# Moving the stores of an inverse transform from GpSimd's queue to SyncE's

## The chip, the cores and the metric

The kernel runs on one core of a Trainium2 chip. The metric is the device time of one execution in microseconds, and the time given is the median of several executions. Profiles are of one execution each. In their rows PE is TensorE's matmul, PEld its weight load, DVE is VectorE, ACT is ScalarE, POOL is GpSimd and SP is SyncE; SP does no arithmetic and serves to issue transfers.

## The reference

The input x has 16 samples of 16 channels of 256 x 256 float32. Four layers follow each other, and each adds a convolution of the normalised input to the input (normalised: by group of two channels, over a sample).

```python
x = x + _L0_conv_ref(_gn(x), L0_conv_weight)      # 3x3, circular
x = x + _L1_conv_ref(_gn(x), L1_conv_filter_w)    # 5 taps on a diagonal
x = x + _L2_conv_ref(_gn(x), ty, tx, pole1, pole2, residue)
x = x + _L3_conv_ref(_gn(x), w_int8, scale, bias) # 3x3 on quantised input
```

Layer 2 is the one that matters here. It takes a 2-D Fourier transform of its input, mixes the channels at every frequency, transforms back, and adds a second term that is made of exponentials of learned poles over the two axes:

```python
alpha = jnp.fft.fft2(x, axes=(-2, -1))
output_residue1 = jnp.einsum('biox,oxik->bkox', alpha, S)
x1 = jnp.fft.ifft2(output_residue1, s=(Ny, Nx), axes=(-2, -1)).real
F = jnp.einsum('kbpq,bipz->kbiqz', output_residue2, E1)
x2 = jnp.einsum('kbiqz,biqx->kizx', F, E2).real
return x1 + x2 / Nx / Ny
```

Layer 3 quantises its normalised input by the largest absolute value of the whole tensor, so that nothing of it can start before all of layer 2's result is known.

## The kernel before

The program runs in stages, and each keeps its result in DRAM for the next: layers 0 and 1 (result `x2d`), the forward transform, the mixing of channels (result `mixd`), the inverse transform (result `x3d`, which is the sum of `x2d` and layer 2), and layer 3 (result `out`). The change is in the inverse transform.

That stage has 128 iterations. The outer loop runs over pairs of channels (`k` = 0, 2, ... 14), the inner one over the 16 samples `b`; one iteration makes one sample's two output channels, 128 partitions of 4 rows of 256. Numbered through, iteration n is `k` = 2 (n // 16), `b` = n % 16. The steps of an iteration are:

- `ot` (L1111): the mixed frequencies of eight samples, loaded at every eighth iteration by 16 transfers of 256 KB on SP's queue; two buffers.
- `xt` (L1118): the part of `x2d` to which the result is added, one transfer of 512 KB on SP's queue; four buffers.
- `along_y` (L1066): 64 small matmuls on PE into `ps_z` (three PSUM buffers), copied by ACT to `zt` (L1069).
- `ps_f` (L1123): one matmul with the exponentials, copied by ACT to `fs` (L1125).
- `along_x`, which PE does one iteration late, for the sample before: 32 matmuls into `ps_o` (L1078, L1079; three PSUM buffers), copied by ACT to `rq` (L1080; three buffers). From there POOL makes `w` (two operations) and half of `o`, DVE the other half (all of these are recorded at line L190, that of a helper). DVE then adds `o` into `xt` and keeps the largest value (`mx`, L1090), and takes statistics (`bn_stats` at L1094, `bn_aggr` at L1095) and the smallest value (`mn`, L1096).
- the store: POOL issues the transfer of `xt` to `x3d` (L1097), 512 KB.

The call `exponentials(k + 2)` stands in the program at `b` = 4 of each round of 16. It gives ACT, DVE and POOL (`dex`, `du`, `da`, `exp` in the rows) a few operations each, in the course of a round.

Only PE's order is written out by hand (`manual_schedule`). The order on the other engines and on SP's queue is made by a scheduler at build time, from the program's order and its own estimates. At run time every engine and every queue goes through its instructions in order: one that waits holds up all behind it. On SP that means loads of `ot` and of `xt` in one sequence. A load of `xt` can be issued when the store of four iterations before has landed, for it takes over that buffer.

After the last iteration the scales of layer 3 are made from the statistics (from L1138), and layer 3 loads `x3d` with SP (L1234) and stores `out` with POOL (L1270).

Of the kernel before, what the change touches and what calls it, by code (L numbers as in the profile page):

```python
# [57 lines left out]
P = 128  # L58
# [106 lines left out]
def layers(ctx, tc, x, w0, w1, w3, sw, bias, ty, tx, p1a, p1b, p1c, p2a, p2b, p2c, resa, resb,  # L165
           const, rows, out):
    nc = tc.nc
# [8 lines left out]
    x3d = [x3p[b // 2][b % 2] for b in range(B)]  # L176
# [12 lines left out]
    def tt(eng, o, a, b, op):  # L189
        eng.tensor_tensor(o, a, b, op)  # L190

    V, Q = nc.vector, nc.gpsimd
# [20 lines left out]
    def strip_weights(pool, src, taps, dtype, name, parts):  # L213


        raw = pool.tile([P, taps, C], F32, tag=f"{name}r", name=f"{name}r")
        nc.sync.dma_start(raw, src)
        n = sum(c for _, _, c, _ in parts)
        w = pool.tile([P, n, C * S], dtype, tag=name, name=name)
        for to, frm, count, m in parts:  # L220
            for i in range(count):
                tt(Q, w[:, to + i, :].rearrange("p (o s) -> p o s", s=S), bc(raw[:, frm + i, :], 2, S),
                   bc(strip[:, m, :], 1, C), MUL)
        return w
# [454 lines left out]
    with ExitStack() as es:  # L679
# [17 lines left out]
        with ExitStack() as tmp:  # L697
# [3 lines left out]
            for m, (t, pole) in enumerate(((ty, p1b), (tx, p2b))):  # L701
                rs = over_step(tp, t, f"b{m}")
                w = tp.tile([P, 2], F32, tag=f"wn{m}", name=f"wn{m}")
                V.tensor_scalar(w, nat, rs, TWO_PI, MUL, MUL)
                pr, pi, h = (tp.tile([P, C * KP], F32, tag=k, name=f"{k}{m}") for k in ("pr", "pi", "h"))
# [295 lines left out]
    with ExitStack() as es:  # L1001
# [28 lines left out]
        def exponentials(k):  # L1030


            made, turns = [], []
            for m in range(2):
                ex, u = (ap_.tile([P, 2, N], F32, tag=f"{n}{m}", name=f"{n}{m}") for n in ("dex", "du"))
                pr, pi = poles_[m]
                for d in range(2):
                    nc.scalar.activation(ex[:, d], times[m], AF.Exp, scale=pr[:, k + d : k + d + 1])
                    nc.scalar.activation(u[:, d], times[m], AF.Identity, bias=quarter, scale=pi[:, k + d : k + d + 1])
                turns.append((ex, u))  # L1040
            for m, (ex, u) in enumerate(turns):

                a = ap_.tile([P, 2, N], F32, tag=f"da{m}", name=f"da{m}")
                V.tensor_scalar(a, u, ROUND, ROUND, ADD, SUB)
                tt(Q, u, u, a, SUB)
                nc.scalar.activation(a, u, AF.Sin, scale=BELOW_TWO_PI)
                if m:
                    V.scalar_tensor_tensor(ex, ex, sign, a, MUL, MUL)
                else:
                    tt(V, ex, ex, a, MUL)  # L1050
                e = ep.tile([P, 2, 2, P], F32, tag=f"exp{m}", name=f"exp{m}")
                for s_, op_ in enumerate((ADD, SUB)):
                    tt(V, e[:, :, s_, :], ex[:, :, 0:P], ex[:, :, P:N], op_)
                made.append(e)
            return made
# [4 lines left out]
        def along_y(b, d, ot):  # L1060

            ps = ps_z.tile([P, 2, 2, P], F32, tag="ps_z", name="ps_z")
            for a, c in cells:
                for t in range(4):
                    r, half = t // 2, t % 2
                    nc.tensor.matmul(ps[32 * t : 32 * t + 32, a, c, :], lhsT=ot[:, a, d, 2 * c + half, r, b % BD],  # L1066
                                     rhs=inv[:, a, r], start=True, stop=True)
            zt = tp.tile([P, 2, 2, P], F32, tag="zt", name="zt")
            nc.scalar.copy(zt, ps)  # L1069
            return zt  # L1070

        def along_x(b, k, zts, fs, ey, xt):

            rq = rp.tile([P, 2, 2, 2 * P], F32, tag="rq", name="rq")
            for d in range(2):
                ps = ps_o.tile([P, 2, 2, P], F32, tag="ps_o", name="ps_o")
                for a, c in cells:
                    nc.tensor.matmul(ps[:, a, c, :], lhsT=zts[d][:, a, c, :], rhs=last[:, c, :], start=True, stop=False)  # L1078
                    nc.tensor.matmul(ps[:, a, c, :], lhsT=fs[:, d, a, :], rhs=ey[:, d, c, :], start=False, stop=True)  # L1079
                nc.scalar.copy(rq[:, d], ps.rearrange("p a c x -> p a (c x)"))  # L1080
            w = zp.tile([P, 2, 2, 2 * P], F32, tag="w", name="w")
            for h, op_ in enumerate((ADD, SUB)):
                tt(Q, w[:, :, h], rq[:, :, 0], rq[:, :, 1], op_)
            o = zp.tile([P, 2, 2, 2, P], F32, tag="o", name="o")
            parts_ = w.rearrange("p d h (c x) -> p (d h) c x", c=2)
            for h, (eng, op_) in enumerate(((V, ADD), (Q, SUB))):
                tt(eng, o[:, :, :, h, :].rearrange("p d h x -> p (d h) x"), parts_[:, :, 0], parts_[:, :, 1], op_)
            at = b * (C // 2) + k // 2
            flat = xt.rearrange("p d h w -> p (d h w)")
            V.tensor_tensor_reduce(flat, flat, o.rearrange("p d h c x -> p (d h c x)"), 1.0, -3.0e38, ADD, ALU.max,  # L1090
                                   mx3[:, at : at + 1])
            st = small.tile([P, 2, 6], F32, tag="st3", name="st3")
            for d in range(2):
                V.bn_stats(st[:, d], xt[:, d].rearrange("p h w -> p (h w)"))  # L1094
            V.bn_aggr(mv3[:, at, :], st.rearrange("p d s -> p (d s)"))  # L1095
            V.tensor_reduce(mn3[:, at : at + 1], flat, AX.X, ALU.min)  # L1096
            Q.dma_start(x3d[b][k : k + 2].rearrange("c (h p) w -> p c h w", p=P), xt)  # L1097

        with tc.manual_schedule(engines={mybir.EngineType.PE}):
            before = None  # L1100
            exps = exponentials(0)
            for k in range(0, C, 2):
                for b in range(B):
                    if b % BD == 0:

                        ot = op.tile([P, 2, 2, 4, 2, BD, 32], F32, tag="ot", name="ot")
                        for a in range(2):
                            for d in range(2):
                                for r in range(2):
                                    for u in range(2):  # L1110
                                        nc.sync.dma_start(  # L1111
                                            ot[64 * u : 64 * u + 64, a, d, :, r].rearrange("p t b g -> p t (b g)"),
                                            mixd[64 * a : 64 * a + 64, :, k + d, (r + u) % 2, u, b : b + BD]
                                            .rearrange("q t b g -> q t (b g)"))
                    if b == 4:
                        coming = exponentials(k + 2) if k + 2 < C else None
                    xt = xp.tile([P, 2, 2, N], F32, tag="xt3", name="xt3")
                    nc.sync.dma_start(xt, x2d[b][k : k + 2].rearrange("c (h p) w -> p c h w", p=P))  # L1118
                    zts = [along_y(b, d, ot) for d in range(2)]

                    fs = fp.tile([P, 2, 2, P], F32, tag="fs", name="fs")
                    ps = ps_f.tile([P, 512], F32, tag="ps_f", name="ps_f")
                    nc.tensor.matmul(ps, lhsT=gall[:, b, :], start=True, stop=True,  # L1123
                                     rhs=exps[0].rearrange("p k a y -> p (k a y)"))
                    nc.scalar.copy(fs.rearrange("p k a y -> p (k a y)"), ps)  # L1125
                    if before:
                        along_x(*before)
                    before = (b, k, zts, fs, exps[1], xt)
                    if k == C // 2 and b == 0:
                        wt = strip_weights(last_, w3, 9, BF16, "wt3", [(0, 0, 9, 0), (9, 0, 3, 1), (12, 6, 3, 2)])  # L1130
                exps = coming
            along_x(*before)


        tp = es.enter_context(tc.tile_pool(name="d_s", bufs=1))
# [248 lines left out]
```

## Time and profile before

| what | us |
|---|---|
| runs: median (lowest, highest) | 4475.6 (4469.8, 4476.33) |
| profiled execution, its own time | 4466.67 |
| its span in the profile | 4464.9 |
| first start of the store at L1097 | 3154.8 |
| last start of the store at L1097 | 4053.1 |
| busy in the whole span: PE | 3986.4 |
| busy in the whole span: DVE | 3051.8 |
| busy in the whole span: ACT | 2752.2 |
| busy in the whole span: POOL | 2208.0 |

The median of the runs and the profiled execution are of different executions of the same program; what is worked out from the profile is to be set against the profile's own time. A share of busy time over the whole span is a mean over five stages with different limits, and what is read for one stage has to be taken from a window on that stage. Times within the profile count from the start of the span. "x3d<-xt" in a row means that the instruction writes `x3d` and reads `xt`.

### The profile page before, as it was taken

How to read it: one execution, taken by the hardware profiler on the slowest of the kernel's cores; microseconds unless marked ns; L12 is line 12 of the kernel's file. 1: busy time of each engine (PE TensorE's matmuls, PEld its weight loads, DVE VectorE, ACT ScalarE, POOL GpSimd, SP SyncE). 2: the span in 40 equal slices, each digit the busy share in tenths (PEclk: the TensorE clock that was granted, in tenths of full speed). 3: DMA queues.
4: the chain of work that ended last, by engine and by line, in shares of the span. 5: the costliest groups of instructions: out<-in, count | busy, mean ns of one | idle time of the engine just before them, and what ended most of it. 6: DMA issues, size and time to landing. Idle time of an engine off the chain costs nothing. (4 is left out here: it accounts for less than half of the span.)

```text
span 4464.9 us, 122570 instructions
## 1 busy us (share of the span) xinstructions
PE 3986.4 (89%) x50800; PEld 3069.6 (69%) x50800; DVE 3051.8 (68%) x5654; ACT 2752.2 (62%) x3667; POOL 2208.0 (49%) x3466
## 2 busy tenths in 40 slices
PE   4999999999948999899989999997999999995776
PEld 1555555555527999899967777775778888883444
DVE  4767676767677878787755555554566666767998
ACT  2877777777623444444458888887544444445998
POOL 2242424232345546464556666664677777773222
PEclk9999999999978999999989999998999999997999
DMA  6777776767443545354447777777887878876998
GB/s 144 166 174 168 168 174 163 179 158 183 105 113 103 164 136 172 123 162 153 152 101 166 164 170 166 167 172 173 219 219 219 219 217 230 235 205 240 350 351 310
DMA packets 431340, 820.54 MB, mean 184 GB/s; under 512 B 41600, under 2 KB 306816, under 8 KB 415360
## 3 DMA queue, kind: packets, MB, share of 16 engines
q1 hardware_dynamic: 365248, 577.52, 50.2%
q0 software_dynamic: 65536, 235.18, 16.8%
q8 instruction: 401, 6.57, 0.7%
q14 instruction: 155, 1.27, 0.1%
HBM read 408.85 MB, written 336.07 MB: 167 GB/s over the span
## 5 line engine op out<-in xcount | busy, mean ns | idle before, releaser
L382 PE MATMUL ps<-va,wt 128*64 128x512 f32 (+1 forms) x1632 | 668.9, 571 | 11.4 <-POOL va L354 9.2
L382 PE MATMUL ps<-vb,wt 128*64 128x512 f32 (+1 forms) x1632 | 667.1, 570 | 4.6 <-DMA vb<-va 4.6
L878 ACT COPY sk<-ps_s 64x516 f32<-64x516 f32 x1016 | 593.0, 584 | 117.8 <-PE ps_s L873 98.5
L771 ACT ACTIVATE y<-ps_y,bc 128x384 f32<-128x384 f32 x512 | 297.1, 581 | 423.1 <-PE ps_y L769 423.1
L873 PE MATMUL ps_s<-t,l 128*128 128x258 f32 x2048 | 523.5, 398 | 18.7 <-ACT sk L878 8.1
L190 DVE TENSOR_TENSOR ob<-ps_m,other 128x256 f32<-128x256 f32 x512 | 271.1, 607 | 355.5 <-ACT other L966 350.8
L403 ACT ACTIVATE v<-xt,nm 32x2048 f32<-32x2048 f32 x248 | 497.2, 2005 | 9.8 <-PE ps L417 3.5
L417 PE MATMUL ps<-v,w1s 128*64 128x259 f32 x4096 | 481.8, 395 | 11.0 <-DVE v L401 6.7
L382 PEld LDWEIGHTS ps<-va,wt 128*64 128x64 f32 x1632 | 223.3, 137 | 311.3 <-issue 282.8
L873 PEld LDWEIGHTS ps_s<-t,l 128*128 128x128 f32 x2048 | 372.2, 192 | 93.5 <-ACT sk L878 8.4
L417 PEld LDWEIGHTS ps<-v,w1s 128*64 128x64 f32 x4096 | 337.2, 141 | 133.0 <-issue 24.1
L1079 PE MATMUL ps_o<-exp,fs 128*128 128x128 f32 x2048 | 402.7, 279 | 14.2 <-ACT fs L1125 14.2
L1078 PE MATMUL ps_o<-c_last,zt 128*128 128x128 f32 x2048 | 401.7, 278 | 0.2
L1218 PE MATMUL ps_c<-q,wt 64*64 64x512 bf16 (+1 forms) x4608 | 288.1, 401 | 105.2 <-ACT o L1265 88.1
L1078 PEld LDWEIGHTS ps_o<-c_last,zt 128*128 128x128 f32 x2048 | 327.1, 195 | 63.1 <-issue 62.5
L941 PEld LDWEIGHTS ps_m<-z,sk 128*32 128x32 f32 x16384 | 254.5, 110 | 129.3 <-issue 108.3
L941 PE MATMUL ps_m<-z,sk 128*32 128x64 f32 x16384 | 303.7, 222 | 38.6 <-issue 35.3
L190 POOL TENSOR_TENSOR acc<-acc,prod 128x256 f32<-128x256 f32 x240 | 228.2, 951 | 216.0 <-DVE prod L190 209.3
L190 POOL TENSOR_TENSOR w<-rq 128x512 f32<-128x512 f32 x256 | 320.9, 1280 | 26.2 <-ACT rq L1080 15.4
L1079 PEld LDWEIGHTS ps_o<-exp,fs 128*128 128x128 f32 x2048 | 317.0, 195 | 15.4 <-ACT fs L1125 15.4
L1218 PEld LDWEIGHTS <-wt 64*64 64x64 bf16 x4800 | 179.8, 113 | 213.8 <-issue 144.7
L766 PE MATMUL ps_y<-c_y,qd 128*128 128x128 f32 x2048 | 315.9, 277 | 5.1 <-ACT y L771 5.1
(347 smaller groups left out, 8853.0 us busy)
## 6 DMA issues: line engine op xcount, KB each, us to landing
xt<-x2d SPq DMA_DIRECT2D x256, 512.0 KB, 4.3
z<-alphad SPq DMA_DIRECT2D x516, 129.0 KB, 4.8
xt<-in_x_dram SPq DMA_DIRECT2D x256, 256.0 KB, 7.2
x2d<-x2s POOLq DMA_DIRECT2D x256, 256.0 KB, 5.0
mixd<-ob SPq DMA_DIRECT2D x128, 512.0 KB, 5.8
ot<-mixd SPq DMA_DIRECT2D x256, 256.0 KB, 7.2
x3d<-xt POOLq DMA_DIRECT2D x128, 512.0 KB, 5.7
xt<-x3d SPq DMA_DIRECT2D x64, 1024.0 KB, 8.8
```

Source lines behind the costliest of these rows:

```text
L190: eng.tensor_tensor(o, a, b, op)
L382: nc.tensor.matmul(ps[halves[h], lo:hi, :], lhsT=wt0[:, w, :], rhs=v[:, 2 * t + lo : 2 * t + hi, j : j + N], start=j == 0 and k == 0, stop ...
L403: nc.scalar.activation(to, o.xt[c][q_], AF.Identity, bias=o.g.nm[q_, 1:2])
L417: nc.tensor.matmul(ps[halves[h], k, 0:U], lhsT=o.w1[:, w : w + 64], rhs=v1[:, lo : lo + U], start=first_, stop=not first_)
L766: nc.tensor.matmul(to[:, :, a, :], lhsT=v[:, c, a, i % 2, :], start=a == 0, stop=a == 1, rhs=y1[:, a].rearrange("p (r f) -> p r f", r=2))
L771: nc.scalar.activation(y[:, c, :], ps[:, 0 : 3 * P], AF.Copy, scale=bc2[:, b, i // 2, 0:1])
L873: nc.tensor.matmul(ps[:, d, 0 : 2 * NX], lhsT=ls[h][:, k + d - k0], rhs=t2[:, h, k + d].rearrange("p x r -> p (x r)"), start=True, stop=True)
L878: copy(sks[2 * e8 + n][64 * h : 64 * h + 64, :, 2 * k : 2 * k + 4] .rearrange("p x (k r) -> p x k r", r=2), ps[64 * n : 64 * n + 64, :, 0 ...
L941: nc.tensor.matmul(to, lhsT=sk[:, x_], rhs=z[:, :, x_], start=True, stop=True)
L1078: nc.tensor.matmul(ps[:, a, c, :], lhsT=zts[d][:, a, c, :], rhs=last[:, c, :], start=True, stop=False)
L1079: nc.tensor.matmul(ps[:, a, c, :], lhsT=fs[:, d, a, :], rhs=ey[:, d, c, :], start=False, stop=True)
L1218: nc.tensor.matmul(o, lhsT=wt[half[h], w, :], rhs=src, start=i == 0, stop=i == len(work[0]) - 1)
```

## The change

The store of a finished `xt` is no longer issued by POOL at the end of `along_x`. `along_x` puts it on a list instead. The loop takes it off the list one iteration later, after it has issued the next load of `xt` and the copy to `fs`, and issues it on SP's queue. The two that are left at the end are issued after the loop. Nothing of the arithmetic changes, and the transfers are the same in number and size. Where each store comes to stand on SP's queue is decided by the scheduler.

```diff
             V.bn_aggr(mv3[:, at, :], st.rearrange("p d s -> p (d s)"))
             V.tensor_reduce(mn3[:, at : at + 1], flat, AX.X, ALU.min)
-            Q.dma_start(x3d[b][k : k + 2].rearrange("c (h p) w -> p c h w", p=P), xt)
-
+            stores.append((x3d[b][k : k + 2].rearrange("c (h p) w -> p c h w", p=P), xt))
+
+
+        stores = []
         with tc.manual_schedule(engines={mybir.EngineType.PE}):
             before = None
             exps = exponentials(0)
...
                     nc.scalar.copy(fs.rearrange("p k a y -> p (k a y)"), ps)
+                    if stores:
+                        nc.sync.dma_start(*stores.pop())
                     if before:
                         along_x(*before)
                     before = (b, k, zts, fs, exps[1], xt)
...
             along_x(*before)
+            for store in stores:
+                nc.sync.dma_start(*store)
```

## The prediction

> **What bounds the kernel now.** I read the 40 slices first, then the windows of the stage that the change touches (3130 to 4054 us, the inverse transform), then its waits, its chain and its DMA view.
>
> ```profile
> PE   4999999999948999899989999997999999995776
> POOL 2242424232345546464556666664677777773222
> PEclk9999999999978999999989999998999999997999
> ```
>
> Over the program PE is the busy engine. In the slices of this stage (the 29th to the 36th) POOL is at 6 to 7 tenths beside it, so one view more is needed to see which of the two sets the pace.
>
> ```profile
> 3160.00:3600.00 440.00, 412.62 (x6033) 359.63 (x6035) 294.95 (x452) 203.72 (x348) 314.21 (x264) 0.97 0.82 221
> 3600.00:3740.00 140.00, 131.50 (x1891) 113.75 (x1882) 97.95 (x146) 64.58 (x113) 100.72 (x81) 0.95 0.78 218
> 3740.00:3980.00 240.00, 240.00 (x3602) 210.67 (x3602) 163.47 (x254) 107.96 (x184) 177.85 (x143) 1.00 0.86 233
> ```
>
> Columns: length, busy PE, PE weight load, DVE, ACT, POOL, granted clock, DMA share, GB/s. PE is idle for 27.4 and 8.5 us in the first two and never in the third, at clock 1.00. Its own pace stands in the chain of waits as the distance of two starts of the same work:
>
> ```profile
> 3757.75 1.89 PE ps_z L1066 x64
> 3764.26 1.89 PE ps_z L1066 x64
> ```
>
> That is 6.51 us for one iteration (one sample b, two channels). POOL's pace stands further on in the same chain:
>
> ```profile
> 3918.88 2.51 POOL w L190 x2
> 3921.48 1.78 POOL o L190
> 3923.28 1.22 DVE xt L1090
> 3924.52 0.29 issue
> 3924.81 0.77 POOL x3d L1097
> 3925.60 2.52 POOL w L190 x2
> ```
>
> From w to w it is 6.72 us: 4.29 us of POOL's arithmetic, then POOL stands still for DVE's addition into xt (1.22) and the semaphore (0.29), because the store's issue (0.77) comes before the next w on POOL. Its waits in 3160 to 4054 say the same; it lacks input for only 15.4 us:
>
> ```profile
> POOL x3d L1097 <- DVE mx L1090: 207.7, 125, 2.5
> POOL w L190 <- ACT rq L1080: 15.4, 5, 3.1
> ```
>
> So POOL is the bound, by 0.21 us an iteration over PE, plus the exponentials: every 16 iterations it also makes two du, and the store starts of iterations 4, 20, 36, 52, 68, 84, 100 and 116 (3188.6, 3303.5, 3419.2, 3534.8, 3649.8, 3762.0, 3871.0, 3978.6) lie 115 us apart in four rounds, then 112, 109 and 108, where 16 x 6.72 is 107.5. PE runs ahead until its buffers are full, then stalls. At the end POOL trails: PE's last product ends at 4028.3 (its next one starts at 4055.4 after 27.17 us idle), the last store starts at 4053.1.
>
> **The change, part by part.**
> *POOL loses the store.* Off POOL's queue go the wait (1.22 + 0.29 us) and the issue (0.77): 2.28 of 6.72 us an iteration. What is left, 4.4 us with gaps, hides under PE's 6.51. If DVE and POOL hinder each other (POOL's o takes 1.78 us beside DVE's o, and as little as 1.34 alone), every one of its three operations at 1.78 is 5.3 us, still under 6.51. PE is late next.
> What PE at its own pace gives: from the first ps_f (3138.2) 127 x 6.51 = 826.8 us to the last one, then ps_f with along_x(126) 4.6 us and along_x(127) 3.6 us: 3973.2 us, against 4028.3 now. So 55.1 us of stalls are what can come back. By the starts of ps_f they lie in iterations 17 to 20 (16.4 us), 33 to 36 (11.7), 49 to 52 (9.5), 65 to 68 (11.5) and 81 to 83 (7.0); the odd 1 us is the start-up. From 97 on there are none.
> Behind PE's end the last iteration still needs rq 0.59 + w 2.51 + o 1.78 + DVE 1.22 + 0.29 + gaps 0.3 = 6.7 us to its store, where now it is 24.8: 18.1 us. Both together: 73.2 us.
> *What of the stalls stays.* They sit where the exponentials are made. There ACT, in order, waits for DVE (dex behind exp, 54.5 us in ten waits) and for POOL (da behind du, 33.2 us in eight), and the copies that empty PSUM stand behind it. The first is mostly DVE trailing PE by three or four iterations, and goes with POOL's delay; the second is the way from engine to engine, about 4 us each, and stays. Bounds: 0 (iterations 97 and later) to the 55 us of now. Two waits of 4 us a round, half taken up by the three PSUM buffers of each kind, make 4 us for five and a half rounds: 22. I take 22, nearer to the second row than to either end, and 2 us for the start.
> *SP gains the store.* In the built order of instructions the load of xt for iteration s+4 stands directly behind the store of iteration s, and the store of s+1 behind that; two ot transfers stand between each pair. The load waited for that store before too, as four xt buffers are all there are (SP waited 657.9 us in this stage for x3d). New is the wait of the store on SP for DVE, with ot and load behind it. Who waits for them: PE's ps_z for ot, DVE's L1090 for xt. Counting from the start of an iteration on PE, store s can start at about the start of s+3. The last ot of a group whose first use is iteration 16 stands behind store 11: issued at start(14) + 1, landed 7.2 us later, needed at start(16), which is 13.0 us: 4.8 us to spare. The load: store s lands 5.8 us after its start, load 0.4 + 4.6 us; xt is needed about 24 us after store s started: 13 us to spare. SP's issue time is store 0.36 (as xt's load of the same shape) + load 0.36 + 2 x 0.6 = 1.9 of 6.5 us. All hidden, by these margins.
> *What the store costs on SP's queue.* No SP store of this shape is in the trace. The rows near it:
>
> ```profile
> x3d<-xt POOLq DMA_DIRECT2D x127, 512.0 KB, 5.8
> xt<-x2d SPq DMA_DIRECT2D x124, 512.0 KB, 4.6
> ot<-mixd SPq DMA_DIRECT2D x233, 256.0 KB, 7.2
> mixd<-ob SPq DMA_DIRECT2D x96, 512.0 KB, 5.8
> ```
>
> The last is the stage before. SP becomes a chain: store issue to landing L, then the next load's issue 0.4, then the next store; period L + 0.5. It must stay under 6.51 for PE to set the pace. Lower bound L = 3.6 (the shortest xt load), upper 7.2 (ot's row). The Trainium skill, page "DMA: Bandwidth & Descriptors", section "Queues, rings and completion order", speaks against the change: every DMA engine takes turns between the queues that have work, and all of SP's DMAs share one. So far the store had a turn of its own beside SP's loads; now it stands behind them. By that rule a store issued right behind a load has 512 KB ahead, at this stage's 217 GB/s 2.4 us (an estimate): 5.8 + 2.4 = 8.2, period 8.7, and the stage would end at 3154.8 + 127 x 8.7 = 4260 us, 207 us later. By the rows 5.8 is already the landing with both queues mixed, among them stores in a burst of ot; and where the store waits for DVE, the load ahead has partly gone. I take L = 5.8, period 6.3: hidden, with little to spare.
> The stores also change their pieces: POOL's queue moved 66.59 MB in 18288 packets (3.6 KB each) for 20.9% of the 16 DMA engines, SP's 126.63 MB in 129101 (1.0 KB each) for 57.0%:
>
> ```profile
> q1 hardware_dynamic: 129101, 126.63, 57.0%
> q0 software_dynamic: 18288, 66.59, 20.9%
> ```
>
> At SP's price per MB the stores cost 30.0% in place of 20.9%, and the total rises from 79 to 88%, over a stage cut from 900 to 850 us to 93%. A packet's time holds waiting too, and the stage's slices reach 273 GB/s where 195 MB in 850 us need 229, so I cost it at nothing; its cover is the same margins, and if that is gone it shows as a larger L.
> The sum: 73 - 22 - 2 = 49 us. The profiled execution took 4466.7 us (span 4464.9), 8.9 below the median of the runs, 4475.6. I take the gain off the median: 4427.
>
> **The rivals.**
> *SP's chain takes POOL's place (slower).* For it: the landing of 7.2 us in the row of ot, and the queue rule above. Against it: 4.6 and 5.8 in the rows of the same size. Stores now start 7.07 us apart on average (3154.8 to 4053.1 in 127 steps), so it decides from L = 6.6. At L = 7.2 the stage ends at 3154.8 + 127 x 7.7 = 4132.7 instead of 4053.1: 80 us, 4555.
> *The stalls are the exponentials' own (little changes).* If ACT's waits of 54.5 and 33.2 us come from the order on the engines and not from POOL's delay, PE keeps its 55 us and only some of the tail's 18 comes back, the rest lost to late ot: 4475, or 4458 with the whole tail. For it: all stalls lie there. Against it: PE leads most just before, and POOL, not ACT, is in the chain of waits.
> *All stalls go.* Gain 73: 4402. Against it: da behind du.
>
> **How the numbers follow.** A difference of 0.2% (9 us) is about what a measurement of this kernel tells from none. Forecast with its neighbours on the fast side (4402 to 4458): 0.78, likeliest 4427. Exponentials alone with no gain left: 0.07. SP's chain: 0.15. The range 4400 to 4480 takes in the forecast's bounds and the case without gain, and leaves out most of SP's chain; the likeliest case's own range is 4402 to 4458.
>
> **What would show it.** Right: POOL's groups have no x3d; the store on SP; POOL waits for rq instead of mx; PE at 6.51 us an iteration through most of the stage, stalls of some 4 us a round; 6 to 8 us from PE's last product to the last store; the chain runs over PE. Wrong: PE's ps_z waiting for ot or DVE's L1090 for xt by more than 20 us in all, or a chain of waits that goes store, landing, load, store on SP, with the landing of x3d at 6.6 us or more.

## The result and the profile after

| | before | after |
|---|---|---|
| median of four runs each (lowest to highest), us | 4472.7 (4467.0 to 4476.3) | 4415.0 (4404.2 to 4417.5) |
| profiled execution, its own time / span, us | 4466.7 / 4464.9 | 4417.5 / 4415.1 |
| first to last start of `ps_f`, us | 3138.2 to 4020.0 | 3137.4 to 3984.8 |
| PE's last product of the stage ends, us | 4028.3 | 3993.1 |
| last store of `x3d` starts, us | 4053.1 | 4001.4 |

The ratio of the times is 0.987, with a 95% interval of 0.985 to 0.989: 58 us by the medians, 50 by the two spans. The forecast was 4427, a gain of 49 on the 4475.6 that were known then; the fourth run of the kernel before, 4467.0, moved its median to 4472.7. The spans give the smaller gain because the profiled execution of before is faster than all four of its runs, and that of after is the slowest of its four.

The same slices as before, of the page of the kernel after:

```profile
PE   4999999999957999899989999999699999996777
POOL 2242423233245556464556666665466666663222
PEclk9999999999978999999989999999899999998998
```

POOL loses its 7s in the stage. The windows of the stage (length, busy PE, PE weight load, DVE, ACT, POOL, granted clock, DMA share, GB/s):

```profile
3160.00:3600.00 440.00, 427.33 (x6332) 374.43 (x6334) 309.29 (x483) 219.03 (x374) 294.69 (x216) 0.98 0.84 233
3600.00:3740.00 140.00, 139.95 (x2095) 122.33 (x2084) 102.42 (x158) 64.76 (x113) 95.40 (x66) 1.00 0.83 236
3740.00:3980.00 240.00, 240.00 (x3621) 210.50 (x3620) 168.44 (x263) 108.31 (x185) 156.73 (x112) 1.00 0.81 234
```

PE's idle time falls from 27.4 to 12.7 us in the first window and from 8.5 to 0.05 in the second, by 23 us in all. The granted clock rises too, from 0.97 and 0.95 to 0.98 and 1.00. By these rounded shares PE lacked some 20 us of full clock before (0.03 x 440 + 0.05 x 140) and some 9 after (0.02 x 440), so that about 11 us more come back that way: an estimate.

The chain of waits still goes through POOL's instructions, but in another rhythm:

```profile
3964.20 2.50 POOL w L190 x2
3966.78 1.77 POOL o L190
3968.55 2.12 issue
3970.71 2.51 POOL w L190 x2
```

From `w` to `w` it is 6.51 us, which is PE's own pace, where it was 6.72. The 2.12 us of "issue" is no work of POOL's: it is the time in which POOL has nothing to do until the next `rq`. The waits of 3160 to 3995 us (time in all, times, longest) say so. First two of the kernel before, then the kernel after, its engines and SP:

```profile
ACT dex L1038 <- DVE exp L190: 54.5, 10, 12.4
ACT da L1046 <- POOL du L190: 33.2, 8, 4.7
```

```profile
POOL w L190 <- ACT rq L1080: 253.1, 118, 5.4
ACT da L1046 <- POOL du L190: 32.4, 8, 5.3
ACT dex L1038 <- DVE exp L190: 22.2, 6, 6.1
DVE xt L1090 <- DMA xt<-x2d: 7.0, 6, 1.2
```

```profile
SPq L1120 <- DMA x3d<-xt: 396.9, 118, 6.4
SPq L1129 <- DVE mx L1090: 76.5, 34, 6.1
```

POOL waits for input for 253 us where it was 15; its wait for `mx` (207.7 us up to 4054) is gone. ACT's wait for DVE's `exp` fell from 54.5 to 22.2 us, and its wait for `du` stayed at 32 (33.2 before). PE waits nowhere for `ot` in this stretch, and DVE for `xt` 7.0 us in all. On SP the wait of the new store is put down to `mx` 34 times (76.5 us), and 33 times to other operations of DVE (24.5 us). In the trace 49 of the 128 stores leave within 0.6 us of the end of their `mx`. The others leave up to 4.9 us later; ahead of them on SP stand the loads that wait for the landing of an older store (396.9 us). The landings, of the DMA view of 3160 to 3990 us (issue to landing, median):

```profile
x3d<-xt SPq DMA_DIRECT2D x125, 512.0 KB, 5.4
xt<-x2d SPq DMA_DIRECT2D x123, 512.0 KB, 4.4
ot<-mixd SPq DMA_DIRECT2D x233, 256.0 KB, 6.1
```

Where the 50 us come from, by these times: from first to last `ps_f` it is 847.4 us in place of 881.8, which is 34.4 (23 of idle time and, by the estimate above, some 11 of clock). From PE's end to the last store it is 8.3 in place of 24.8, which is 16.5. The stage begins 0.8 us earlier, and layer 3 behind it takes 413.7 in place of 411.8 us. 34.4 + 16.5 + 0.8 - 1.9 = 49.8.

### The profile page after: what moved, and what is told of

Same layout as the page of the kernel before. It is cut to its first block, busy times and chain, and to the rows that moved or that the text cites. A ratio compares the mean times of both kernels' runs of the same rounds, so it can differ in the third digit from the quotient of the medians.

```text
span 4415.1 us, 122736 instructions
## 1 busy us (share of the span) xinstructions
PE 3972.6 (90%) x50800; PEld 3061.9 (69%) x50800; DVE 3045.7 (69%) x5654; ACT 2750.3 (62%) x3667; POOL 2119.1 (48%) x3338
## 3 DMA queue, kind: packets, MB, share of 16 engines
q0 software_dynamic: 47104, 168.06, 12.7%
## 5 line engine op out<-in xcount | busy, mean ns | idle before, releaser
L190 POOL TENSOR_TENSOR w<-rq 128x512 f32<-128x512 f32 x256 | 332.8, 1321 | 264.0 <-ACT rq L1080 255.3
```

## The experiments

Each ratio is against runs of the kernel before on the same chip (medians of before: 4464.0 to 4469.7 us). "Stalls" are what the starts of `ps_f` show above 6.51 us a step, from the first to the last iteration: 55.1 us before, 20.7 after. A "making" is one call of `exponentials`.

**Is it the queue, or POOL's standing still?** In the first kernel the store stays on POOL, and an ordering edge puts it behind the next iteration's `o`. In the second it is on ACT's queue at the place of the change.

```diff
-                        nc.sync.dma_start(*stores.pop())
...
-                        along_x(*before)
+                        late = along_x(*before)
+                    if len(stores) > 1:
+                        put = Q.dma_start(*stores.pop(0))
+                        tc.add_manual_dep(put.ins if hasattr(put, "ins") else put, (late.ins if hasattr(late, "ins") else late).name,
...
```

> The store goes back to POOL's queue, but stands there behind the next iteration's o instead of behind its own, so that POOL finds DVE's addition already done; it still issues 0.77 us a store. My theory (the change pays because POOL no longer stands still for DVE ahead of its next w): POOL needs 2.51 + 1.78 + 0.77 = 5.1 us of PE's 6.51, so nearly the whole gain: 4415 to 4425 us, POOL's wait for mx under 20 us, PE paces the stage. Rival (the gain is the kind of queue: transfers that SP issues are cheaper than POOL's, or land sooner): as before, 4465 to 4476.

4419.2 us, ratio 0.990 [0.988, 0.991]; stalls 18.1 us, the last store at 4002.0. POOL in the timeline:

```profile
3768.11 2.50 POOL L190 TENSOR_TENSOR w<-rq 128x512 f32<-128x512 f32 x2 [1.44 <-ACT rq L1080]
3770.69 1.77 POOL L1087 TENSOR_TENSOR o<-w 128x512 f32<-128x512 f32 x1
3772.41 0.77 POOL L1132 DMA_DIRECT2D x3d<-xt  x1
3774.62 2.50 POOL L190 TENSOR_TENSOR w<-rq 128x512 f32<-128x512 f32 x2 [1.44 <-ACT rq L1080]
```

The store still costs POOL its 0.77 us, but by the time it comes up DVE has long finished, and POOL is the one that waits for `rq` (1.44 us). By the ratios that is four fifths of the gain (1.04 of 1.31%, with intervals that overlap), had without leaving POOL's queue. What cost the time was, for the most part, the place of the store on an engine that has work to do, directly behind an operation whose result it must wait for.

```diff
-                        nc.sync.dma_start(*stores.pop())
+                        nc.scalar.dma_start(*stores.pop())
```

> The store is issued on ACT's queue in place of SP's, from the same place in the program; in the built order it stands behind fs of iteration s+2 and ahead of both rq copies of s+1. My theory (what counts is what stands behind the waiting store): the copies to rq of s+1 cannot start before DVE has added iteration s, which closes a ring: store 0.4 + two rq 1.2 + w 2.51 + o 1.78 + DVE 1.22 + 0.29 + gaps 0.3 = 7.7 us an iteration. 127 x 7.7 = 978 us of stores against 898 before: slower than before by up to 80 us, 4530 to 4555. Rival (the kind of queue, or any queue but POOL's): as the change, 4405 to 4425.

4514.7 us, ratio 1.011 [1.009, 1.012]: slower than before. ACT stands in the way in POOL's stead:

```profile
ACT rq L1080 <- DVE mx L1090: 416.3, 89, 8.4
```

The median step of PE is 7.27 us: 77 of the 127 steps lie at it, 22 are longer, most of them around the exponentials, and 26 are at PE's own pace. The ring (`rq` on ACT, POOL, DVE, the store on ACT, the next `rq`) forms, but at 7.27 and not 7.7 us, so that the loss of 46 us falls short of the 61 to 86 expected. The two kernels together say that the change works because the store holds up no arithmetic on SP, not because a queue other than POOL's carries the bytes.

**What are the stalls that stay?** The trace of the kernel after shows the one of iteration 36, in which 4.2 us are lost. First ACT, then PE, then the windows' row just behind it (columns as above):

```profile
3373.89 0.63 ACT L1046 ACTIVATE da<-du 128x512 f32<-128x512 f32 x1 [3.41 <-POOL du L190]
3374.42 0.57 ACT L1127 COPY fs<-ps_f 128x512 f32<-128x512 f32 x1
3375.04 0.49 PE L1079 MATMUL ps_o<-exp,fs 128*128 128x128 f32 x2 [2.35 <-ACT fs L1127]
```

```profile
3376.00:3379.00 3.00, 3.00 (x16) 3.00 (x16) 2.87 (x6) 2.88 (x6) 1.99 (x2) 0.50 0.57 172
```

On ACT the copy to `fs` stands behind `da`, which waits 3.41 us for POOL's `du`, and PE waits 2.35 us for `fs`. The other 1.9 us are lost after the wait, while PE is busy at a granted clock of 0.50. ACT's wait for the other `du` of the same making (4.22 us, at 3361 us) holds up PE nowhere. Iterations 52 and 68 show the same: 2.35 us of waiting for 4.2 lost, 3.30 for 5.2.

The experiment makes the exponentials once, in both kernels, and uses them for all eight rounds. Seven of the eight makings are left out, so these kernels do not compute layer 2; the same holds for the other three without the exponentials below.

```diff
-                        coming = exponentials(k + 2) if k + 2 < C else None
+                        coming = exps
```

> The changed kernel with the exponentials made once, for the first pair of channels, and used for all (seven of the eight makings are left out). My theory (the 21 us of PE stalls that are left lie in the rounds of the exponentials, in ACT's waits for POOL and DVE): they go, 4390 to 4400. Rival (they come from SP's chain: ot or xt behind the waiting store): they stay, 4410 to 4418.

4400.8 us, ratio 0.985 [0.984, 0.987]. Not the gain expected (4390 to 4400), and the interval overlaps that of the kernel after. The stalls of each round are gone, but others have come at iterations 48, 56, 80, 88, 104, 112 and 120, all multiples of eight, where a new `ot` is first used (3160 to 3995 us):

```profile
PE ps_z L1066 <- DMA ot<-mixd: 6.2, 6, 3.3
```

> The kernel before with the exponentials made once and used for all. My theory (POOL's 6.72 us an iteration is the bound, and the exponentials come on top): the rounds of 115 us become 107.5, and the end stays on POOL: 35 to 45 us less than before, 4428 to 4440, still some 40 above the changed kernel without exponentials. Rival (the stalls are the exponentials' own, POOL's store costs little): as fast as the changed kernel without exponentials, 4390 to 4405.

4427.0 us, ratio 0.991 [0.989, 0.993], 1 us below the range expected. POOL goes on in its old pace (`POOL x3d L1097` waits 192.8 us for `mx`), with stores 6.81 us apart. PE has stalls at multiples of eight here too (12.2 us of waits for `ot`, with the stores on POOL and the loads on SP waiting for them), so a late `ot` alone does not tell of a chain on SP. Without the exponentials the change is worth 26 us, or 34 with the order on SP that e13 has below; with them it is worth 50 to 58. The two costs, POOL's store and the exponentials, amplify each other.

**Is SP's chain the next bound?** In e4 a store starts 7.6 us (median) after its `mx`. The timeline of SP there:

```profile
3844.99 0.36 SPq L1120 DMA_DIRECT2D xt<-x2d  x1
3845.39 0.52 SPq L1129 DMA_DIRECT2D x3d<-xt  x1
3845.95 1.99 SPq L1113 DMA_DIRECT2D ot<-mixd  x2
3850.74 0.37 SPq L1120 DMA_DIRECT2D xt<-x2d  x1
3851.16 0.50 SPq L1129 DMA_DIRECT2D x3d<-xt  x1
```

The load at 3850.74 leaves when the store of 3845.39 has landed, and the next store leaves 0.42 us after it. Nothing else is waited for: store, landing, load, store. Over iterations 40 to 120 of e4 (the exponentials made once, in the kernel after) the mean of this chain is 5.83 (landing) + 0.06 + 0.70 (load to next store, often with an `ot` issue between) = 6.60 us, which is 0.09 above PE's pace. The transfers of `ot` stand in the same sequence and drift until they arrive too late: the lag of a store behind its `mx` grows from 0 to some 8 us over the first 40 iterations. Three kernels without the exponentials test that. The first takes the stores off SP (the edit of e1):

> The kernel with POOL's store behind the next iteration's o (e1), with the exponentials made once and reused in all eight rounds (seven of eight makings are left out). The counterpart of the kernel after without them, which came to 4400.8 with new waits of PE for ot of some 11 us. Theory (those waits were SP's chain of store, landing, load): here the stores are off SP, so that no wait for ot comes, PE's stalls in the stage are under 3 us, and the time is 4388 to 4394. Rival (the waits for ot come from the load on the DMA engines at PE's full pace, whatever queue the stores are on): the same waits of PE for ot, 4398 to 4404. Third (POOL's own pace of w, o and the store's issue is the next bound): no waits for ot, but PE waits for ps_o or rq, 4395 to 4405.

4397.2 us, ratio 0.983 [0.982, 0.985]: 3 us over the expectation and in the third theory's range, but PE waits for neither `ot` nor POOL in the windows of the stage. It is busy in the whole of the first:

```profile
3160.00:3600.00 440.00, 440.00 (x6641) 385.83 (x6640) 326.82 (x475) 198.35 (x338) 345.63 (x285) 1.00 0.89 243
```

The second keeps the stores on SP and adds a fifth buffer:

```diff
-        xp = es.enter_context(tc.tile_pool(name="d_x", bufs=4))
+        xp = es.enter_context(tc.tile_pool(name="d_x", bufs=5))
```

> The kernel after the change with the exponentials made once and reused in all eight rounds (seven of eight makings are left out), and with five buffers for xt in place of four. With four (e4) it took 4400.8 us, and PE waited for ot by some 10 us at the start of later rounds. Theory (SP's chain: a store, its landing, the load into the same buffer, and with four buffers the next store cannot leave until that load has): a fifth buffer lets each load wait for a store one iteration older, the ot loads leave earlier, and the waits for ot go: stalls in the stage under 2 us, 4390 to 4396. Rival (the DMA engines themselves are too slow at PE's full pace, or the store on SP's queue holds the loads up whatever the buffers): the waits for ot stay, 4399 to 4403.

4404.1 us (4389.0 to 4408.7), ratio 0.985 [0.982, 0.987]: no gain. The stage has 18.7 us of stalls, again at the multiples of eight:

```profile
SPq L1120 <- DMA x3d<-xt: 429.9, 118, 6.9
PE ps_z L1066 <- DMA ot<-mixd: 15.1, 8, 3.6
```

SP waits for landings as long as with four buffers (428.8 us). The order on SP in the traces tells why. With five buffers the scheduler put the load of n+5 where the load of n+4 stood, directly behind store n (120 of 123 loads; in e4 all 124). It waits for the same landing with the same instructions queued behind it. So the third kernel keeps the five buffers and moves the load one store back with an ordering edge:

```diff
+                    if at >= 4:
+                        tc.add_manual_dep(got.ins if hasattr(got, "ins") else got, puts[at - 4].name,
...
```

> The kernel after the change with the exponentials made once and reused in all eight rounds (seven of eight makings are left out), five buffers for xt, and an ordering edge that puts each load of xt on SP behind the store of four iterations before it, one store later than the scheduler put it in e11. In e11 the scheduler used the fifth buffer to move each load one place earlier on SP, directly behind the store whose buffer it takes over, so that the load still waited there for that store's landing with the next store and the ot loads queued behind it. Theory (that wait at the head of SP is the chain, and PE's waits for ot in e4 and e11 are its cost): SP's wait of loads for x3d falls from 430 us to under 100, the waits for ot go, stalls in the stage are under 2 us, and the time is 4390 to 4397 against 4400.8 for e4 and 4404 for e11. Rival (the three transfers of an iteration on one kind of queue are what delays ot, whoever waits): the waits for ot stay at 6 us or more and the time at 4399 to 4405.

4393.0 us (4388.1 to 4397.2), ratio 0.983 [0.981, 0.985]. The chain is gone, and with it the waits of PE for `ot`. First SP's waits, then its timeline, then the windows:

```profile
SPq L1134 <- DVE mx L1090: 454.7, 125, 8.1
SPq L1120 <- DMA x3d<-xt: 0.5, 2, 0.3
```

```profile
3840.56 0.37 SPq L1134 DMA_DIRECT2D x3d<-xt  x1
3841.02 0.45 SPq L1120 DMA_DIRECT2D xt<-x2d  x1
3841.52 2.43 SPq L1113 DMA_DIRECT2D ot<-mixd  x3
3847.07 0.37 SPq L1134 DMA_DIRECT2D x3d<-xt  x1
```

```profile
3160.00:3600.00 440.00, 440.00 (x6610) 386.45 (x6612) 301.67 (x473) 197.90 (x338) 295.28 (x218) 1.00 0.94 246
```

The stores now leave 6.51 us apart, in step with PE. From the third `ot` on, the last transfer of each lands 4.8 to 6.3 us before the iteration that first uses it starts on PE; in e4 and e11, from iteration 48 on, it lands 0.9 to 5.2 us after that start in all but one case. The intervals of e4, e11 and e13 overlap, so the times alone would not decide it; from first to last `ps_f` the profiles have 836.4, 845.5 and 825.4 us, and the waits name the cause. The rival, that the loads of `ot` and `xt` and the stores together are too much for one queue or for the DMA engines at PE's pace, falls: they are carried at a share of 0.94.

**Can the exponentials' stalls be taken away?** First by moving the subtraction `du` from POOL to DVE, in the kernel after and in e1.

```diff
-                tt(Q, u, u, a, SUB)
+                tt(V, u, u, a, SUB)
```

> The kernel after the change, with the subtraction of the rounded turns (du, two instructions of 128x512 each eight rounds) on DVE in place of POOL. In the kernel after, ACT waits 33.9 us in 10 places for that du, and PE is idle 20.7 us around the exponentials. Theory of a cushion (the exponentials' stalls are POOL's standing in their way, but the chain of stores and loads on SP stands just behind and catches up in each of those pauses): ACT's wait falls to under 10 us, PE's stalls around the exponentials fall by some 10 us, and about half of that comes back as waits of PE for ot: 4405 to 4412 us. Rival (SP's chain has room enough): the whole 10 to 15 us show, 4400 to 4405, with no wait for ot above 4 us in the stage. Second rival (the exponentials' stalls come from ACT's own 12 instructions and not from POOL): no change, 4412 to 4418.

4411.1 us, ratio 0.987 [0.985, 0.988]: the same as the kernel after (0.987). Stalls 18.1 us in place of 20.7.

```profile
ACT dex L1038 <- DVE exp L190: 53.2, 10, 8.5
ACT da L1046 <- DVE du L190: 9.5, 4, 3.1
```

The time lies in the range of the first expectation and 1 us below that of the third (no change), which the ratio supports; neither gave the reason. ACT's wait for `du` did fall from 32.4 to 9.5 us, but its wait for DVE's `exp` rose from 22.2 to 53.2. The work went to the engine on which the next wait depends. PE had no wait for `ot` in this stretch.

> The kernel with POOL's store behind the next iteration's o (e1), and the same subtraction on DVE. Here the store waits for nothing on SP and ot comes 13 us or more before its use, so that no chain of SP's can give the gain back. Theory of a cushion: more comes through than in the kernel after with the same edit, 4402 to 4410 against 4419 without it, PE's stalls from 18 to under 8 us. Rival (SP's chain had room enough): the gain is the same in both, within 4 us.

4425.8 us, ratio 0.990 [0.989, 0.992], against 0.990 [0.988, 0.991] of e1: no gain either, and stalls of 33.9 in place of 18.1 us in its profile. The theory of a cushion is not supported: it would have had the stalls here under 8 us.

Then by making the exponentials in two parts, at `b` = 4 and `b` = 10 (so that fewer of their operations come at one place), in the kernel after, in e1, and in the kernel after with five buffers.

```diff
-        def exponentials(k):
+        def exponentials(k, which=(0, 1)):
...
-                        coming = exponentials(k + 2) if k + 2 < C else None
+                        coming = exponentials(k + 2, (0,)) if k + 2 < C else None
+                    if b == 10 and coming:
+                        coming = coming + exponentials(k + 2, (1,))
```

> The kernel after the change, with the next round's exponentials made in two parts: those along y at the fifth sample of a round, those along x at the eleventh, in place of all at the fifth. In the kernel after, one making holds up PE by 4.5 us a round (20.7 us in all) because ACT meets twelve more instructions at one place and waits for du and for DVE's exp. Theory (the size of the burst makes the stall, and half a burst fits into what PE's buffers ps_o and ps_z ahead of ACT can take up): stalls of 1 us or less at either place, about 15 us less of stall; SP's chain, which has no pauses left to catch up in, gives back 5 to 10 of it at PE's waits for ot: 4402 to 4410 us. Rival (each half holds up PE as long as the whole, since it is the wait for another engine's answer that counts): 4412 to 4422. Second rival (no chain of SP's in the way): 4397 to 4402.

> The kernel with POOL's store behind the next iteration's o (e1), with the exponentials in the same two parts. No chain of SP's stands behind the stalls here. Theory (size of the burst): stalls from 18.1 to under 5 us, no waits for ot, 4400 to 4408 us against 4419 for e1. Rival (each half stalls as long as the whole): 4415 to 4425.

> The kernel after the change with both: the exponentials in two parts and five buffers for xt. This one computes all, and is what the experiments point to as faster than the kernel after. Theory (burst size and SP's chain are the two that are left): stalls of PE in the stage under 6 us, no wait for ot above 3 us in all, 4398 to 4406. Rival (each half stalls as long as the whole): 4412 to 4420, the same as with four buffers.

4416.2 us (ratio 0.989 [0.987, 0.991]), 4420.7 (0.990 [0.988, 0.992]) and 4413.5 (0.988 [0.986, 0.990]): as without the edit. They decide nothing about the size of the burst, for the scheduler moved the second part up to where it had stood. In the traces of after and e9 the order of the stage is the same on POOL and SP, and on ACT and DVE it differs only in a few operations of the exponentials at its start, before 3143 us. Behind that ACT begins the exponentials at the same times within 2 us (at 3349, 3457 and 3566 us in both). Whether a shorter burst would stall PE less is open; it needs ordering edges, as the place in the program did nothing. No kernel that computes everything was measurably faster than the kernel after.

## Why the prediction was right

- *The bound.* "POOL is the bound, by 0.21 us an iteration over PE, plus the exponentials": shown. With the store's wait off POOL, even with the store still on POOL (e1), POOL waits for `rq` and its step is PE's 6.51 us.
- *PE's recoverable stalls, 55.1 us, and 22 of them staying.* 20.7 stay. The split was right in its direction: the wait of `dex` for `exp` fell from 54.5 to 22.2 us with POOL's delay, and that of `da` for `du` stayed (33.2 to 32.4). It was right too that of the two waits of a round one is covered, and that `da` behind `du` makes the rest: the rows of iteration 36 show it. But that the size came out was in part luck. PE waits 2.35 us there, not 4; the 1.9 us at half clock that make up the 4.2 are a term that the prediction did not have. The 55.1 held it as well: PE was idle for only 35.9 of them in the windows of before. Nor is that wait all that can hold PE up: e6 takes most of it away, the wait for `exp` comes in its place, and the stalls stay. Only leaving the makings out took them away (e8 and e13). A slip: the five groups of stalls in the list add up to 56.1 and not 55.1 us, for a step of PE is 6.50 rather than 6.51 (825.4 / 127 in e13).
- *The tail, 6.7 us from PE's end to the last store.* It is 8.3, so 16.5 came back in place of 18.1. In the chain the last `w` starts 1.44 us after PE's end (forecast: 0.59 for `rq`) and takes 3.46 us (2.51); `o` takes 1.26 (1.78). The 1.34 us that the prediction calls "alone" were measured beside DVE's `exp`; with nothing beside it, `o` took 1.26 in the kernel before too.
- *SP's store, L = 5.8 us, "hidden, with little to spare".* The median is 5.4 us, and it is hidden; `xt` had 12.4 us to spare (median; forecast 13), `ot` 2.6 to 7.0 us in most groups (forecast 4.8). But the step "period L + 0.5 = 6.3" was too small. The free chain takes 6.60 us (e4), over PE's 6.51, because the mean landing is 5.83 and the way from load to next store 0.70. It costs nothing in the kernel after: store starts lie 0 to 4.9 us behind their `mx`, and this lag goes back to 0 around each pause of PE at the exponentials. In the 44 iterations after the last pause it stays under 4.6 us; why it does not grow there is open. So the first rival of the forecast, SP's chain, is wrong for this kernel and right once the exponentials are out of the way: at PE's pace it decides from a landing of 6.51 - 0.76 = 5.75 us, and not from 6.6.
- *The queue rule.* The Trainium skill, page "DMA: Bandwidth & Descriptors", section "Queues, rings and completion order", has every DMA engine take turns between the queue rows that have work, and the 8.2 us of the prediction were an estimate from that. In the kernel after 5.4 was measured, against 5.8 for the store with POOL's queue to itself in e1 and 5.0 on ACT's (e2, at a slower pace): a turn of its own was worth no more than 0.4 us in these runs. The turns themselves no run here shows. The order on the queue does count: in e13, where the load stands behind the store, the store lands in 3.9 us and the load takes 6.6, against 5.5 and 4.5 in e11, whose code lacks only the ordering edge. Being second goes with 1.6 to 2.1 us more.

```profile
x3d<-xt SPq DMA_DIRECT2D x126, 512.0 KB, 3.9
xt<-x2d SPq DMA_DIRECT2D x123, 512.0 KB, 6.6
```

- *The DMA share, 79 to 88 or 93%, costed at nothing.* Costing it at nothing was right (e13: 0.94, with PE never idle). The rise itself hardly came. Over 3160 to 3980 us, first before, then after:

```profile
q1 hardware_dynamic: 124581, 121.82, 60.5%
q0 software_dynamic: 16560, 60.30, 20.8%
q1 hardware_dynamic: 193054, 189.80, 82.2%
```

The two queues took 81.3% before, and SP's alone takes 82.2% after, with 4% more bytes. A MB on SP's queue cost 13% less than before, so that the price of one profile did not carry over to the next, as the prediction warned.
- *"The chain runs over PE."* It runs over POOL's `w` and `o` and the gap between, in PE's step. This sign did not come; the step was the thing to read, not the names in the chain.
- *The sum of 49.* By the spans it is 49.8. That the two meet is in part luck: the stalls gave 34.4 us (forecast 55.1 - 22 - 2 = 31.1), the tail 16.5 (18.1), start and layer 3 together -1.1 (0).

## What to carry to other kernels

A store belongs on an engine with nothing else to do, or, if it stays on one that computes, behind the next piece of that engine's work instead of directly behind the result that it waits for: the two came within 0.3% of each other here. Once it is on a queue with the loads, read the chain store, landing, load, next store as a loop with its own period, and compare that with the bound's pace: a fifth buffer did not break it, the fifth buffer with the load moved one store back did. Count a stall by the lost steps and not by the idle time alone: here PE's waits of 2.35 us cost 4.2. And look at the order in the trace before reading a null result: an edit that the scheduler undoes tests nothing.

## What the runs showed of the hardware

With SP's waits for landings gone, the 16 DMA engines ran at a share of 0.94 over 440 us (e13) with PE busy for all of it; the landing of `ot` was 6.8 us, against 6.1 in the kernel after. The landing of a 512 KB store went with its place beside the load of the same size: 5.4 us behind the load on SP's queue (5.5 in e11), 3.9 ahead of it (e13), 5.0 on ACT's queue (e2) and 5.8 on POOL's (e1). And behind the waits of 2.35 to 3.30 us that PE has at the exponentials in the kernel after, its granted clock stood at 0.50 for 3.4 us each.
